# Sixteen transposed tiles, single sign tiles and a new reckoning of the order in a four-layer graph network

## The chip, the cores and the metric

The kernel runs on one core of a Trainium2 chip. The metric is the time of one execution on the device, in microseconds (us). The time before is the median of three runs.

## The reference

Sixteen graphs of 1024 nodes with 64 features go through four residual layers. Each layer normalises its input, applies a ReLU and adds what a graph layer makes of it, with the same adjacency matrix `adj` of 1024 x 1024 each time (about 0.8% of it off the diagonal is not zero). Layers 0, 1 and 2 use dense products with `adj`; layer 2 uses it twice. Layer 3 asks only which neighbours a node has, thins the list of nodes with more than ten, and takes a weighted sum of three quantiles over what is left.

```python
h = relu(layernorm(x)); x = x + einsum(einsum(adj, h), W0)                 # layer 0: one product with adj
h = relu(layernorm(x)); m = relu(relu(h @ W1 + b1) @ W2 + b2)              # layer 1
msg = relu(einsum(adj, m)); x = x + GRU(msg, h)                            #   one product with adj
h = relu(layernorm(x)); T1 = einsum(adj, h); T2 = 2 * einsum(adj, T1) - h  # layer 2: two products with adj
x = x + (K0 * h + K1 * T1 + K2 * T2) @ weight + bias
h = relu(layernorm(x)); adj_d = dilate_adj(adj, mask)                      # layer 3
agg = sum(w * quantile(h of the neighbours in adj_d, tau)) over tau = 0.25, 0.5, 0.75
x = x + (relu((h + agg) @ W1 + b1) @ W2 + b2) * mask
```

## The kernel before

The work of a graph goes through several Python generators, each of which yields operations one after the other (`run`, L1333). A planner, `Weave`, takes all generators side by side and decides in which order the operations are issued. On the chip each engine then works through its own queue in that order, and semaphores make it wait for results of the others. The planner's time is a reckoning only: `Line.cost` (L306) gives each operation a cost, for which it takes its engine, and a delay (`later`) after which its result is there. `Weave.run` (L432) picks the engine that can start something first, and on it, among the operations that could start within `SLACK` = 0.1 us of that, the one whose generator has the lowest key. An operation's key holds for all that its generator issues, DMA loads on SP's queue included.

The generators, for graph b:

- `transposing` (L862), key b - 3: loads eight column blocks of `adj` (512 KB each, on SP's queue, two `block` buffers), transposes each in eight 128 x 128 pieces on PE, and has ACT copy the two PSUM banks into one tile of the stock `AT`. Eight `AT` tiles hold the transposed matrix of one graph. The stock has `AT` = 15 of them.
- `coding` (L664), key b + `CODE_KEY` = b - 3: takes the sign of each `AT` tile on ACT (fp16, tile `there`, two signs in one tile), clears the diagonal on DVE, and packs the neighbours of each node into words by matmuls. The words go through the tile `words`, are transposed and become `code`.
- `lists` (L696), key b - 2: makes each node's list of up to 24 neighbours from `code`, mostly on DVE (`MAX8`, `MATCH_REPLACE8`), and thins it.
- `layers` (L927), key b - 3: layers 0 to 2 and the norm of layer 3. It has four passes over the eight `AT` tiles (`into`, L937; sixteen matmuls a pass). The fourth pass gives each `AT` tile back, once its sign has been taken. Two generators `layering` (L1116) share the graphs, even and odd, and graph b begins when graph b - 1 has done its first pass. At the end the results go into a tile of the stock `pay` (3 tiles), and from there into the DRAM tensors `table` and `rows`, both on SP's queue. Behind them in that queue come the load of the next `X` (two tiles) and further blocks.
- `gathering` (L1122), key b + 1: 80 indirect DMAs on POOL (10 neighbours x 8 tiles of nodes) that read rows of `table` into one of two tiles `G`.
- `quantiling` and `dense` (L1151, L1264), keys b + 1 and b: a sorting network on DVE over the gathered cells, weights on DVE and ACT, the two small matrix products on PE, the store of the output, and the return of the `pay` tile.

After graph 15 the few nodes with longer lists are taken together (`MANY`, 122 gathers in four groups, then 9 scatters).

Of the kernel before, what the change touches and what calls it, by code (L numbers as in the profile page):

```python
# [10 lines left out]
F32 = mybir.dt.float32  # L11
F16 = mybir.dt.float16
# [4 lines left out]
AF = mybir.ActivationFunctionType  # L17
# [5 lines left out]
P = 128  # L23
N = 1024
NT = N // P
C = 64
NB = 64
S = N // NB
# [70 lines left out]
EXTRA = 6 * NT  # L99
BIG = 1e30  # L100
SLACK = 0.1
GATHER = 1.33
RANK = 3.0
SHARE = 3
LONGEST = 512
AT = 15
XTILES = 2
PAYS = 3
LIST_KEY = -2
CODE_KEY = -3  # L110
WORDS = NB - 1
LAYERS = 5
CAND = WORDS + 8 * LAYERS
UNIT = 2.0 ** -10
# [65 lines left out]
def network(n, places, beam=200):  # L180
# [4 lines left out]
    for layer in needed(batcher(n), range(places)):  # L185
        new = {}
        for buf, (cost, ops) in states.items():
            classes = {}
            for a, b, la, lb in layer:
# [73 lines left out]
class Op:  # L263
# [5 lines left out]
    def __init__(self, line, make, writes, reads, cost, later=0.0, after=()):  # L269
        self.line, self.make, self.cost, self.later, self.after = line, make, cost, later, after  # L270
        self.writes, self.reads = [place(a) for a in writes], [place(a) for a in reads]
# [16 lines left out]
class Line:  # L288
# [17 lines left out]
    def cost(self, method, out, reads, kwargs):  # L306
        if method == "dma_start":
            return 0.4, 2.0 + out.nbytes() / 150e3
        n = max(a.free_size() for a in [out] + reads)
        extra = "accum_out" in kwargs  # L310
        if self.name == "DVE":
            fixed = {"match_replace": 0.145, "max": 0.155}.get(method, 0.155)
            return fixed + n / 960 + 0.08 * extra, 0.0
        if self.name == "ACT":
            scalars = sum(hasattr(kwargs.get(k), "ap") for k in ("bias", "scale"))
            return 0.225 + n / 1400 + 0.09 * scalars + 0.19 * extra, 0.0
        if self.name == "PE":
            if method == "transpose":
                return 0.19, 0.25
            n = out.free_size()  # L320
            if mybir.dt.size(reads[0].dtype) == 2:
                return 0.06 + n / (4400 if out.shape[0] == C else 2200), 0.3
            pair = n == 512 and reads[0].shape[0] == P and out.shape[0] == C
            return (0.58 if pair else max(0.34, 0.06 + n / 545)), 0.3
        return 1.33, 2.2


class Weave:
# [13 lines left out]
    def stock(self, name, tiles):  # L342
        self.stocks[name] = list(tiles)

    def give(self, name, t):
        self.stocks[name].append(t)
# [121 lines left out]
class Fast:  # L468
# [4 lines left out]
    def __init__(self, tc, half, whole, weights):  # L473
# [107 lines left out]
        def stock(name, count, shape, dtype=F32):  # L581
            weave.stock(name, [p.tile(shape, dtype, name=f"{name}{i}") for i in range(count)])
# [6 lines left out]
        weave.stock("fm", banks[5:8])  # L589


        stock("there", 2, [P, 2, N], F16)
        stock("code", 1, [P, NT, NB])
        self.words = p.tile([P, 512], F32, name="words")
        self.top = p.tile([P, NT, WORDS], F32, name="top")
        self.cand = p.tile([P, NT, CAND], F16, name="cand")
        stock("L", 3, [P, NT, LIST], F16)
# [3 lines left out]
        stock("block", 2, [P, NT, P])  # L601
        stock("AT", AT, [P, N])
        stock("X", XTILES, [P, NT, C])
# [27 lines left out]
    def gather(self, out, table, at, reads):  # L631

        def make():
            return self.nc.gpsimd.indirect_dma_start(  # L634
                out=out, out_offset=None, in_=table, in_offset=bass.IndirectOffsetOnAxis(ap=at, axis=0))
        return Op(self.G, make, [out], [reads, at], GATHER, 2.2)

# [26 lines left out]
    def coding(self):  # L664

        V, T, S = self.V, self.T, self.S
        for b in range(GRAPHS):
            yield float(b) + CODE_KEY
            yield lambda: self.turns > 0
            bank = yield "bits"  # L670
            turned = self.turned[b]
            for j in range(0, NT, 2):
                there = yield "there"
                for i in range(2):
                    yield lambda: len(turned) > j + i
                    yield S.activation(there[:, i, :], turned[j + i], AF.Sign)
                self.masked[b] = j + 2
                own = there.rearrange("p i (t m) -> p (i t) m", m=P)[:, j:j + NT + 2:NT + 1, :]
                yield V.tensor_mul(own, own, self.noteye[:, None, :].to_broadcast([P, 2, P]))
                for i in range(2):  # L680
                    for half in range(2):
                        yield T.matmul(bank[half * NB:(half + 1) * NB, :], self.bits[:, (j + i) * NB:(j + i + 1) * NB],
                                       there[:, i, 512 * half:512 * half + 512], start=j + i == 0, stop=j + i == NT - 1)
                self.weave.give("there", there)
            yield S.activation(self.words, bank, AF.Identity, bias=self.low, scale=1.0 / UNIT)
            self.weave.give("bits", bank)
            bank = yield "tp"
            for q in range(4):
                yield T.transpose(bank[:, q * P:(q + 1) * P], self.words[:, q * P:(q + 1) * P], self.ident)
            code = yield "code"  # L690
            yield S.activation(code.rearrange("p (h q) w -> p q h w", h=2),
                               bank.rearrange("p (q h w) -> p q h w", h=2, w=NB), AF.Copy)
            self.weave.give("tp", bank)
            self.coded[b] = code
# [95 lines left out]
    def longest(self):  # L790
# [5 lines left out]
        for _ in range(3):  # L796
            tiles.append((yield "AT"))
        run = tiles[0][:, 0:BINS * Q]
# [59 lines left out]
        for t in tiled:  # L858
            self.weave.give("AT", t)


    def transposing(self, adj):  # L862

        D, T, S = self.D, self.T, self.S
        blocks = {}


        early = self.early

        def load(i):  # L870
            b, j = divmod(i, NT)
            blocks[i] = block = early.pop(0).rearrange("p (t m) -> p t m", m=P) if 2 <= i < NT else (yield "block")
            queue = self.A if i % 2 and i < NT else D
            yield queue.dma_start(block, adj[b, :, j * P:(j + 1) * P].rearrange("(t p) m -> p t m", p=P))

        total = GRAPHS * NT
        yield -1.0
        for i in range(NT):
            yield from load(i)
        for i in range(total):  # L880
            b, j = divmod(i, NT)
            yield float(b) - 3
            if NT <= i + 1 < total:
                yield from load(i + 1)
            block = blocks.pop(i)
            at = yield "AT"
            for half in range(2):
                bank = yield "tp"
                for q in range(4):
                    yield T.transpose(bank[:, q * P:(q + 1) * P], block[:, 4 * half + q, :], self.ident)  # L890
                yield S.activation(at[:, 512 * half:512 * half + 512], bank, AF.Copy)
                self.weave.give("tp", bank)
            if not 2 <= i < NT:
                self.weave.give("block", block)
            self.turned[b].append(at)
# [31 lines left out]
    def layers(self, w, b, x):  # L927
# [9 lines left out]
        def into(bank, h, last=False):  # L937

            def step(j):
# [6 lines left out]
                if last:  # L946
                    yield lambda: self.masked[b] > j
                    give("AT", turned[j])
            return step
# [575 lines left out]
def general_layers(tc, b, x, adj, nodemask, VT, mB, X, H, maskT, c16, ident, ones16, ones_row, eps,  # L1525
# [3 lines left out]
    with tc.tile_pool(name="g1", bufs=1) as p1, tc.tile_pool(name="g2", bufs=2) as p2, \  # L1529
# [16 lines left out]
        def neighbours(g):  # L1546
            AT = p2.tile([P, NT, N], F32, name="AT")
            CN = p1.tile([P, NT, N], F16, name="CN")
# [434 lines left out]
```

## Time and profile before

| | |
|---|---|
| median of three runs | 2125.57 us (2113.96 to 2135.73) |
| the profiled execution | 2138.34 us, its span 2136.4 us |
| granted PE clock over the span | 0.782 |
| first gather of graph 0 | 130.9 us after the start |
| last gather of graph 15 | 1898.0 us |
| waits of DVE for `X` loads | 81.4 us, 16 times |
| POOL's gathers | 1402, 0.94 us each in the median |

The profile gives busy times for each engine: PE (matmuls), PEld (weight loads, which overlap PE), DVE, ACT and POOL. SP only issues DMAs. Matrix products in fp32 stand in the trace as two instructions each. A line of the timeline gives the start in us, the length, the engine, the source line, the operation, the tiles written and read (without their numbers), their shape, how many such instructions were merged, and in brackets how long the engine was idle before and what it is thought to have waited for. Nearly all operations carry L303, the line of the planner's wrapper, so they are told apart by their tiles. The clock column is the share of full speed that PE was granted.

### The profile page before, as it was taken

To read this page: it belongs to the slowest core of one execution; us is meant where nothing else is said; L and a number is where in the kernel's file an instruction comes from. 1 tells how busy PE (TensorE), PEld (TensorE's weight loads), DVE (VectorE), ACT (ScalarE), POOL (GpSimd) and SP (SyncE) were. 2 spreads that over 40 slices of the span, in tenths; PEclk is the share of its full clock that TensorE was granted. 3 is DMA by queue.
4 is the path that set the end of the run, shared out by engine and by line. 5 is a ranking of instruction groups with operands and counts; after the bars stand their busy time and mean duration, and the time that the engine had idled before them with its cause. 6 is when DMAs were issued, how large, how long until landed. Compare 5 with 4: busy or idle time off the path is not lost. (4 is left out here: it accounts for less than half of the span.)

```text
span 2136.4 us, 22993 instructions
## 1 busy us (share of the span) xinstructions
PE 1533.9 (72%) x6172; PEld 717.0 (34%) x6172; DVE 1632.9 (76%) x4293; ACT 1073.5 (50%) x2921; POOL 1437.7 (67%) x1441
## 2 busy tenths in 40 slices
PE   6978677869787879787887878787978872233303
PEld 2443323333434343343333333334343331111302
DVE  2661687978888887888886969787788899949646
ACT  3654647566666655566656474757466532011000
POOL 2047776777676767577777667676757777776772
PEclk9979796978788796989796979787779786555555
DMA  4242625252625252444334353525252314121110
GB/s 121 70 86 57 117 38 94 59 105 52 104 51 104 52 93 58 58 94 61 88 62 94 50 94 61 104 48 99 51 92 50 43 31 41 30 31 24 32 27 11
DMA packets 246840, 140.93 MB, mean 66 GB/s; under 512 B 76048, under 2 KB 223952, under 8 KB 246704
## 3 DMA queue, kind: packets, MB, share of 16 engines
q1 hardware_dynamic: 195664, 88.11, 18.4%
q0 software_dynamic: 46096, 48.62, 17.5%
q10 hardware_dynamic: 4944, 2.66, 0.5%
q8 instruction: 53, 0.87, 0.2%
q14 instruction: 83, 0.68, 0.1%
HBM read 120.10 MB, written 19.17 MB: 65 GB/s over the span
## 5 line engine op out<-in xcount | busy, mean ns | idle before, releaser
L634 POOL DMA_INDIRECT G<-table,pay x1402 | 1408.0, 1004 | 652.6 <-issue 351.6
L303 PE MATMUL bank<-AT,nodes 128*64 128x512 f32 x2048 | 605.7, 671 | 88.1 <-ACT nodes L303 78.6
L303 PEld LDWEIGHTS bank<-AT,nodes 128*64 128x64 f32 x2048 | 181.6, 153 | 386.2 <-issue 223.6
L303 PE MATMUL bank<-G,c 128*128 128x512 f32 (+3 forms) x382 | 172.1, 590 | 183.4 <-DVE G L303 179.4
L303 PE MATMUL bank<-c,block 128*128 128x128 f32 x976 | 223.5, 349 | 106.8 <-DMA block<-in_adj 60.5
L303 ACT ACTIVATE AT<-bank 128x512 f32<-128x512 f32 x256 | 149.5, 588 | 188.9 <-PE bank L303 186.4
L303 PEld LDWEIGHTS bank<-c,block 128*128 128x128 f32 x976 | 147.3, 176 | 229.2 <-issue 137.7
L303 DVE TENSOR_TENSOR G<-G 128x512 f32<-128x512 f32 (+3 forms) x313 | 200.1, 674 | 2.8
L303 ACT ACTIVATE nodes<-X,off,ri 128x64 f32<-128x64 f32 x360 | 141.0, 429 | 42.6 <-DVE off L303 41.3
L303 DVE TENSOR_TENSOR net<-G 128x512 f32<-128x512 f32 (+6 forms) x240 | 150.6, 672 | 11.3 <-ACT G L303 9.3
L303 PEld LDWEIGHTS bank<-G,c 128*128 128x128 f32 x382 | 72.1, 226 | 254.5 <-DVE G L303 129.1
L303 ACT ACTIVATE G<-G,coef 128x64 f32<-128x64 f32 x384 | 98.2, 336 | 110.0 <-DVE coef L303 109.8
L303 ACT ACTIVATE sq<-X,st 128x64 f32<-128x64 f32 x360 | 124.6, 346 | 49.7 <-DVE st L303 34.1
L303 ACT ACTIVATE there<-AT 128x1024 f16<-128x1024 f32 x128 | 132.1, 1050 | 0.9
L303 ACT ACTIVATE wide<-bank 64x512 f32<-64x512 f32 x128 | 75.1, 586 | 108.7 <-PE bank L303 107.5
L303 DVE TENSOR_TENSOR G<-net 128x512 f32<-128x512 f32 (+7 forms) x189 | 117.2, 667 | 0.7
L303 DVE TENSOR_TENSOR G<-G,net 128x512 f32<-128x512 f32 (+3 forms) x177 | 111.4, 679 | 0.9
L303 PE MATMUL bank<-wide,wg 64*64 64x512 f32 (+1 forms) x192 | 110.1, 656 | 0.8 <-ACT wide L303 0.4
L303 DVE SCALAR_TENSOR_TENSOR G<-bad,G 128x512 f32<-128x512 f32 (+1 forms) x176 | 109.8, 693 | 0.0
L303 DVE MAX8 L<-cand 128x8 f16<-128x103 f16 x384 | 91.9, 263 | 8.8
L303 PE MATMUL bank<-there,c 128*64 128x512 f16 x256 | 79.8, 449 | 24.3 <-DVE there L303 24.1
L303 DVE TENSOR_REDUCE st<-X 128x8 f32<-128x512 f32 x48 | 32.9, 686 | 82.5 <-DMA X<-in_x 81.4
(200 smaller groups left out, 2235.0 us busy)
## 6 DMA issues: line engine op xcount, KB each, us to landing
block<-in_adj SPq DMA_DIRECT2D x121, 512.0 KB, 4.2
G<-table,pay POOLq DMA_INDIRECT x1402, 2.8
rows<-pay SPq DMA_DIRECT2D x16, 632.0 KB
table<-pay SPq DMA_DIRECT2D x16, 264.0 KB, 5.2
X<-in_x SPq DMA_DIRECT2D x16, 256.0 KB, 8.5
out<-yo SPq DMA_DIRECT2D x16, 256.0 KB, 2.6
G<-in_adj SPq DMA_DIRECT2D x3, 512.0 KB, 10.7
G<-in_adj ACTq DMA_DIRECT2D x3, 512.0 KB, 9.2
```

Of the source, the lines that this page charges most:

```text
L303: return Op(self, lambda: f(*args, **kwargs), writes, reads, cost, later)
L634: return self.nc.gpsimd.indirect_dma_start(out=out, out_offset=None, in_=table, in_offset=bass.IndirectOffsetOnAxis(ap=at, axis=0))
```

## The change

The stock `AT` grows from 15 to 16 tiles of 4 KB per partition. The stock `there` goes from two tiles for two signs each to three tiles for one sign each, and `words` is no longer a tile of its own but borrows one of `there`. Signs, masking and matmuls then go tile by tile, with a masking multiply for each tile in place of one for each pair.

The planner reckons most operations shorter: with DVE and ACT the time until the result is there moves out of the cost into the delay. On PE transposes and fp32 products get cheaper, and a gather goes from 1.33 to 1.29. The key of `coding` goes from b - 3 to b - 2, that of `transposing` from b - 3 to b - 2.5; all others stay.

```diff
-GATHER = 1.33
+GATHER = 1.29
...
-AT = 15
+AT = 16
...
-CODE_KEY = -3
+CODE_KEY = -2
...
         if self.name == "DVE":
-            fixed = {"match_replace": 0.145, "max": 0.155}.get(method, 0.155)
-            return fixed + n / 960 + 0.08 * extra, 0.0
+            fixed = {"match_replace": 0.165, "max": 0.095}.get(method, 0.07)
+            return fixed + n / 960 + 0.08 * extra, 0.09
         if self.name == "ACT":
             scalars = sum(hasattr(kwargs.get(k), "ap") for k in ("bias", "scale"))
-            return 0.225 + n / 1400 + 0.09 * scalars + 0.19 * extra, 0.0
+            return 0.13 + n / 1400 + 0.09 * scalars + 0.19 * extra, 0.1
         if self.name == "PE":
             if method == "transpose":
-                return 0.19, 0.25
+                return 0.165, 0.25
...
-            return (0.58 if pair else max(0.34, 0.06 + n / 545)), 0.3
+            return (0.51 if pair else max(0.26, 0.06 + n / 640)), 0.3
...
-        stock("there", 2, [P, 2, N], F16)
+        stock("there", 3, [P, N], F16)
         stock("code", 1, [P, NT, NB])
-        self.words = p.tile([P, 512], F32, name="words")
...
-            for j in range(0, NT, 2):
+            for j in range(NT):
                 there = yield "there"
-                for i in range(2):
-                    yield lambda: len(turned) > j + i
-                    yield S.activation(there[:, i, :], turned[j + i], AF.Sign)
-                self.masked[b] = j + 2
-                own = there.rearrange("p i (t m) -> p (i t) m", m=P)[:, j:j + NT + 2:NT + 1, :]
-                yield V.tensor_mul(own, own, self.noteye[:, None, :].to_broadcast([P, 2, P]))
-                for i in range(2):
-                    for half in range(2):
-                        yield T.matmul(bank[half * NB:(half + 1) * NB, :], self.bits[:, (j + i) * NB:(j + i + 1) * NB],
-                                       there[:, i, 512 * half:512 * half + 512], start=j + i == 0, stop=j + i == NT - 1)
+                yield lambda: len(turned) > j
+                yield S.activation(there, turned[j], AF.Sign)
+                self.masked[b] = j + 1
+                own = there[:, j * P:(j + 1) * P]
+                yield V.tensor_mul(own, own, self.noteye)
+                for half in range(2):
+                    yield T.matmul(bank[half * NB:(half + 1) * NB, :], self.bits[:, j * NB:(j + 1) * NB],
+                                   there[:, 512 * half:512 * half + 512], start=j == 0, stop=j == NT - 1)
                 self.weave.give("there", there)
-            yield S.activation(self.words, bank, AF.Identity, bias=self.low, scale=1.0 / UNIT)
+            there = yield "there"
+            words = there.bitcast(F32)
+            yield S.activation(words, bank, AF.Identity, bias=self.low, scale=1.0 / UNIT)
...
-                yield T.transpose(bank[:, q * P:(q + 1) * P], self.words[:, q * P:(q + 1) * P], self.ident)
+                yield T.transpose(bank[:, q * P:(q + 1) * P], words[:, q * P:(q + 1) * P], self.ident)
+            self.weave.give("there", there)
...
-            yield float(b) - 3
+            yield float(b) - 2.5
```

## The prediction

> **What bounds the kernel now.** I read the busy times first, then the gather queue, then the stretch between two graphs. The page names no full engine:
>
> ```profile
> PE 1533.9 (72%) x6172; PEld 717.0 (34%) x6172; DVE 1632.9 (76%) x4293; ACT 1073.5 (50%) x2921; POOL 1437.7 (67%) x1441
> L634 POOL DMA_INDIRECT G<-table,pay x1402 | 1408.0, 1004 | 652.6 <-issue 351.6
> ```
>
> POOL is nearer its limit than 67% says: of its 652.6 us idle, 351.6 are the 0.3 us between two gathers that wait for nothing. Gathers in full flow start 1.25 us apart. The longer waits stand where a graph's gathers begin, as between graphs 3 and 4 (POOL's timeline):
>
> ```profile
> 556.46 0.95 POOL L634 DMA_INDIRECT G<-table,pay  x1 [0.30 <-ACT sq L303]
> 566.65 0.94 POOL L634 DMA_INDIRECT G<-table,pay  x1 [9.25 <-DVE below L303]
> ```
>
> The releaser named is wrong: SP issued graph 4's store of `table` at 560.21, such a store lands 5.2 us later, and the gathers follow. Graph by graph, the 80 gathers begin at 130.9, 231.2, 342.8, 452.1, 566.7, 676.1 and so on to 1792.5 (graph 15). That is 1661.6 us for 15 steps, 110.8 each. From first to last, one graph's gathers take 99.0 us in graph 0 and 103.8 on average in graphs 1 to 15; with one interval of 1.25 a step could take 105. The sum of what is lost between graphs is 93 us. So the layers, which end with the table, set the pace, not POOL.
>
> What sets the layers' pace shows in ACT's timeline, at the evictions into `AT` (sixteen to a graph, two to a tile; those of graph 6 run from 561.4):
>
> ```profile
> 618.64 0.57 ACT L303 ACTIVATE AT<-bank 128x512 f32<-128x512 f32 x1
> 620.68 0.58 ACT L303 ACTIVATE AT<-bank 128x512 f32<-128x512 f32 x1
> ...
> 653.05 0.60 ACT L303 ACTIVATE AT<-bank 128x512 f32<-128x512 f32 x1 [9.99 <-PE bank L303]
> 654.76 0.60 ACT L303 ACTIVATE AT<-bank 128x512 f32<-128x512 f32 x1
> ```
>
> Graph 6's seventh tile is done at 621; its eighth stands for 32 us, until graph 5's fourth pass on PE (from 642.78) gives its first tile back. With 15 tiles, 8 + 7 are all there is. Graph 6's first pass needs the eighth tile, so its second, third and fourth passes come after graph 5's fourth, and graph 7's eighth tile after those. The eighth tiles of graphs 5 to 8 come at 544.2, 653.0, 765.3, 881.9: 109 to 117 apart, the step of the gathers. This is a closed loop through one missing tile.
>
> The rows by gather period (length, then PE, PEld, DVE, ACT and POOL busy, clock) show that no engine is full:
>
> ```profile
> 130.90:231.20 100.30, 79.14 (x322) 38.24 (x322) 37.82 (x153) 57.09 (x147) 75.88 (x81) 0.77 0.44 81
> 566.70:676.10 109.40, 90.51 (x368) 41.90 (x368) 91.72 (x244) 67.86 (x185) 80.24 (x80) 0.84 0.40 77
> 787.00:904.90 117.90, 99.15 (x365) 42.26 (x364) 92.16 (x247) 69.53 (x196) 78.32 (x80) 0.78 0.41 72
> ```
>
> DVE has 17.7 us idle in the second row, ACT 41.5.
>
> **The change, part by part.** *Sixteenth `AT` tile.* It adds 4 KB per partition; `there` shrinks from 8 to 6 KB and `words` (2 KB) goes, so space is even. Graph 6's sixth tile was finished at 612, its seventh at 618.6 to 621, 6.6 us on. An eighth at that spacing comes at 627 instead of 653: 26 us earlier. From X load (561.3) to table (781.3) graph 6 took 220 us, two graphs in flight; 220 - 26 = 194, or 97 per step. Three others are late next. POOL: 105, above. The `pay` tiles: graph 3's output store is issued at 738.0, 294.9 after its table (443.1), landing takes 2.6, and graph 6 first writes that tile 14.1 before its own table; 311.6 over three graphs is 103.9. DVE: 91.7 of work, plus whatever in-order waits remain. If all 17.7 us of them remain, the step stays at 109.4 and nothing is won. So the gain lies between 0 and 93. I take 62 (a step of 106.7, DVE idle down to 15): DVE's dependable waits, such as 81.4 us over the run for the X loads, remain, but much of the rest is waiting on chains that the loop itself held back.
>
> *Signs in single tiles.* The signs stay 128. The masking multiplies go from 64 of 128x256 (287 ns, 18.4 us busy) to 128 of 128x128. Their price lies between that of a 128x64 subtraction (`more<-more,top`, 220 ns) and 287: 28 to 37 us, so +10 to +18 over the run. I take 13, nearer to the smaller shape, 0.8 per graph, inside DVE's idle; uncovered it costs 13. The words borrow a `there` tile from eviction to the last of four transposes; code 5 was out at 556.9 and graph 6's first sign came at 577.9, so nobody waits: 0, or up to 5 per graph if signs then follow at once (I take 0).
>
> *New reckoning.* It changes no instruction's length, only the order on each in-order queue. It comes closer to what runs:
>
> ```profile
> 612.57 2.53 DVE L303 TENSOR_TENSOR G<-G 128x512 f32<-128x512 f32 x4
> ```
>
> Four take 2.53 and one 0.69, so they start 0.61 apart. The old reckoning says 0.688, the new 0.603 and 0.09 to the result. By the old one DVE's 244 instructions of a graph look some 20 us longer than they are, and the order is laid out around a full DVE that isn't full. No row shows the new order. The kind of wait that an order makes or removes is DVE's for `ri<-sd` (66.7 us over the run, 37 times), so I bound the edit by 67 won and 67 lost, and take 0: such waits lie in DVE's idle, which isn't the limit while tables come late.
>
> *Later keys.* Transposing moves behind its own graph's layers (b - 2.5 against b - 3), with its SP block loads; coding falls to b - 2. Behind a delayed sign on ACT nobody critical is queued; behind code b waits list b on DVE, and behind that the `pay` of graph b. For graph 5 the list is done at 593.0 and `pay` first written at 655.0: 62 us of cover. Price 0; without cover, microsecond for microsecond. The head (first gather 130.9) and the tail (238 us from graph 15's last gather to the end) I leave alone; the two final gather periods hold 7.7 + 26.1 us of idle DVE to take work pushed into them, so the tail could cost up to 34, or give 13.
>
> *Two rules.* Graph 0's gathers ran 1.253 us apart with DVE busy 37.8 of 100.3, the later ones 1.314 with DVE at about 91. The Trainium skill (SBUF — State Buffer, "SBUF: two separate sides") has it that certain DVE instructions lock GpSimd out of a shared port while it writes descriptors for gathers. By that rule a denser DVE would not leave POOL at its best pitch: 1.253 would make the step 100, while the row's 1.314 makes the 105 I use. Second, PE ran at clock 0.50 from 564 to 598, after a wait of 7.49 us for a block load, then at 1.00. The skill (TensorE: Matmul & The Clock Gate, Part 1) says idle of about 3.4 us halves the clock; by it no single price for a matmul, old or new, can be right on both sides of such a gap. The change doesn't remove the X and block loads behind each table, so I count on no better clock.
>
> **Sum.** The profiled execution took 2138.3 (span 2136.4); the median of three is 2125.6, or 0.994 of it. 2138.3 - 62 = 2076.3; times 0.994 is 2064.
>
> **Rivals.** *The step is held by lists (slower).* Coding falls behind layers, transposing and older work, signs slip on ACT, and `pay` waits for the list. With tables 26 us earlier the cover is 36, and the chain is back at 220 once signs slip by 62; beyond that it is slower than now. At 70 it is 194 + 34 = 228: a step of 114, +3.2 x 15 = +48, 2173 in the median's scale. For: three edits push coding back. Against: ACT idles 41.5 a graph, and eight signs need 8.4.
> *DVE and `pay` take over at once.* Quantiles rank last; if the output lags 16 us more, 327.6/3 = 109.2 per step: -24, or about 2102. For: 103.9 leaves little room. Against: part of the lag is waiting.
> *It doesn't do what it says.* The eighth tile is planned behind the other graph's fourth pass anyway, now that transposing ranks lower: no gain, 2126. Against: PE was idle 5.12 us at 627, and the planner fills idle time.
>
> **How the numbers follow.** A measurement can't tell less than 1% (2104 to 2147) from no change. Forecast 62%: 2064, own range 2020 (93 + 13 won) to 2100. DVE and `pay`: 16%, half of it faster by 1%, half within. Not done: 6%. Lists: 16%. Faster 0.70, same 0.14, slower 0.16. The range of 2015 to 2135 holds all cases but the slower one, the 67 lost by order included (2131); of the 67 won it leaves the last 18 out.
>
> **What would show it.** The eighth tile within 10 us of the seventh; tables some 107 apart; waits at a graph's first gather falling from 93 to about 30 in sum; DVE still about 92 a graph. I am wrong if the step stays at 110 with the eighth tile early (then look at lists, `pay` and DVE's idle), or if the tail after graph 15's last gather grows by tens of microseconds.

## The result, and the profile after

The changed kernel takes 2182.31 us in the median of four runs (2178.42 to 2189.26), beside 2126.7 (2113.96 to 2135.73) for the one before: 1.027 of it, 95% interval 1.0208 to 1.0332. The forecast was 2064, in a range of 2015 to 2135. It was wrong in sign.

The profiled execution took 2186.15 us with a span of 2184.2, 47.8 more than before (2136.4). The starts of the gathers divide the difference:

| us | before | after | |
|---|---|---|---|
| first gather of graph 0 | 130.9 | 141.4 | +10.5 |
| 15 steps, from there to graph 15's first gather | 1661.6 | 1704.4 | +42.8 |
| from there to the end | 343.9 | 338.4 | -5.5 |
| in the steps: waits between two graphs, sum | 93.1 | 58.1 | -35.0 |
| in the steps: first to last gather, sum over graphs 0 to 14 | 1549.8 | 1627.5 | +77.7 |

The two rows on the steps leave out one interval of 1.25 us per step. So what stood between the graphs shrank, as forecast, though not as far as to 30. What the forecast didn't have is that the gathers of one graph now take longer from the first to the last. The gathers themselves got no longer (995 ns in the mean, before 1004): over graphs 0 to 14 the waits beyond the usual 0.3 us between a graph's first and last gather sum to 89 us, before 4.

The stores of `table` divide the 47.8 in another way. The first is 10.1 us later, the 15 steps from there to graph 15's table take 1659.2 us (before 1649.9), and graph 15's gathers begin 51.2 behind their table (before 17.3). So the layers lose little pace, 9.3 us in 15 steps, and most of the loss is that the gathers fall behind the tables.

The page's busy times and gather row of the changed kernel:

```profile
PE 1570.6 (72%) x6172; PEld 683.8 (31%) x6172; DVE 1638.3 (75%) x4357; ACT 1077.4 (49%) x2924; POOL 1425.5 (65%) x1441
L633 POOL DMA_INDIRECT G<-table,pay x1402 | 1395.4, 995 | 711.3 <-issue 344.7
```

DVE works 5.4 us more over the run, POOL 12 less, and POOL is idle 59 us more. Where it waits stands in POOL's timeline, at three gathers with a long wait in brackets. The first begins graph 4, the second graph 8; the third comes after the first eight of graph 9:

```profile
572.08 0.98 POOL L633 DMA_INDIRECT G<-table,pay  x1 [9.11 <-DVE G L303]
...
1030.25 1.15 POOL L633 DMA_INDIRECT G<-table,pay  x1 [13.94 <-DVE net L303]
...
1174.73 0.97 POOL L633 DMA_INDIRECT G<-table,pay  x1 [20.08 <-PE bank L303]
```

SP's timeline has the tables of graphs 8 and 9, and after them the output store of graph 7:

```profile
1015.12 0.37 SPq L639 DMA_DIRECT2D table<-pay  x1
...
1123.43 0.37 SPq L639 DMA_DIRECT2D table<-pay  x1
...
1232.32 0.38 SPq L639 DMA_DIRECT2D out<-yo  x1
```

Graph 4's gathers follow their table (store issued at 565.9) by 6.2 us, as before. Graph 8's table was issued at 1015.1, and the gathers come 15.1 later; graph 9's wait 20 us after the first eight, until 51 after their table. They wait for the tile `G`, which the quantiles of two graphs earlier still use: graph 7's output is not stored before 1232.3. On average over graphs 2 to 14 the gathers begin 20.7 us behind the table's store (before 6.4) and the output is stored 303.4 behind it (before 283.9).

The evictions into `AT` in ACT's timeline, the last of graph 6:

```profile
664.24 1.06 ACT L303 ACTIVATE AT<-bank 128x512 f32<-128x512 f32 x2
669.58 1.05 ACT L303 ACTIVATE AT<-bank 128x512 f32<-128x512 f32 x2
672.38 0.60 ACT L303 ACTIVATE AT<-bank 128x512 f32<-128x512 f32 x1 [0.47 <-PE bank L303]
673.83 0.59 ACT L303 ACTIVATE AT<-bank 128x512 f32<-128x512 f32 x1
```

The eighth tile is done 4 us after the seventh (before, 34 us). But the eighth is not earlier: it ends at 674, and ended at 655 before (107 us behind the load of its graph's `X`, before 94). The seventh, which ended at 621, has moved back to 671. The hole was filled from the wrong side.

The gather periods of graphs 0, 4 and 6 (length, then PE, PEld, DVE, ACT and POOL busy, clock):

```profile
141.40:241.90 100.50, 81.99 (x320) 35.12 (x319) 40.02 (x160) 56.93 (x147) 76.09 (x81) 0.79 0.41 80
572.10:675.80 103.70, 87.44 (x351) 36.56 (x350) 85.89 (x239) 64.29 (x176) 78.14 (x81) 0.88 0.39 76
789.90:910.90 121.00, 100.35 (x400) 44.05 (x398) 92.24 (x252) 75.09 (x210) 78.53 (x80) 0.87 0.45 85
```

Graph 6's period is 121.0 long with DVE at work for 92.2, so DVE stands idle for 28.8. The waits that DVE's idle time is put down to (us in total, times, longest), before:

```profile
DVE st L303 <- DMA X<-in_x: 81.4, 16, 7.9
DVE ri L303 <- ACT sd L303: 66.7, 37, 9.0
DVE cand L303 <- ACT cand L303: 37.2, 13, 3.8
...
DVE there L303 <- ACT there L303: 35.2, 9, 15.6
...
DVE of_h L303 <- ACT wide L303: 23.8, 6, 10.4
```

And after:

```profile
DVE there L303 <- ACT there L303: 78.8, 29, 16.6
DVE st L303 <- DMA X<-in_x: 76.8, 15, 8.1
DVE of_h L303 <- ACT wide L303: 58.6, 11, 15.1
DVE ri L303 <- ACT sd L303: 49.1, 19, 8.8
```

DVE's waits for a sign on ACT have doubled, and so has the gated layer's wait (`of_h`); the waits for `ri` and `cand` went down. In the 14 steps from graph 1 to graph 15 DVE was busy 1291.8 of 1561.3 us before, and 1309.5 of 1603.9 after: 18 us more work in that stretch and 25 us more idle.

### The profile page after: what moved, and what is told of

Its sections match the earlier page's. It is cut to its first block, busy times and chain, and to the rows that moved or that the text cites. A ratio compares the mean times of both kernels' runs of the same rounds, so it can differ in the third digit from the quotient of the medians.

```text
span 2184.2 us, 23009 instructions
## 1 busy us (share of the span) xinstructions
PE 1570.6 (72%) x6172; PEld 683.8 (31%) x6172; DVE 1638.3 (75%) x4357; ACT 1077.4 (49%) x2924; POOL 1425.5 (65%) x1441
## 5 line engine op out<-in xcount | busy, mean ns | idle before, releaser
L633 POOL DMA_INDIRECT G<-table,pay x1402 | 1395.4, 995 | 711.3 <-issue 344.7
L303 PE MATMUL bank<-AT,nodes 128*64 128x512 f32 x2048 | 638.2, 664 | 91.4 <-ACT AT L303 73.1
L303 PE MATMUL bank<-G,c 128*128 128x512 f32 (+3 forms) x382 | 196.3, 648 | 210.2 <-DVE G L303 207.8
L303 PEld LDWEIGHTS bank<-AT,nodes 128*64 128x64 f32 x2048 | 168.1, 149 | 395.6 <-issue 210.9
L303 PE MATMUL bank<-c,block 128*128 128x128 f32 x976 | 196.3, 315 | 30.7 <-DMA block<-in_adj 20.1
L303 PEld LDWEIGHTS bank<-c,block 128*128 128x128 f32 x976 | 119.8, 155 | 231.8 <-issue 186.8
L303 ACT ACTIVATE nodes<-X,off,ri 128x64 f32<-128x64 f32 x360 | 147.3, 429 | 46.7 <-DVE off L303 46.3
L303 PE MATMUL bank<-wide,wg 64*64 64x512 f32 (+1 forms) x192 | 102.3, 620 | 3.4 <-ACT wide L303 3.2
L303 PE MATMUL bank<-c,nodes 128*64 128x128 f32 x128 | 42.9, 361 | 68.0 <-ACT nodes L303 67.4
```

Source lines behind the costliest of these rows:

```text
L303: return Op(self, lambda: f(*args, **kwargs), writes, reads, cost, later)
L633: return self.nc.gpsimd.indirect_dma_start(out=out, out_offset=None, in_=table, in_offset=bass.IndirectOffsetOnAxis(ap=at, axis=0))
```

## The experiments

Each part of the change was first run alone, and then taken out of the whole. A ratio is always to the kernel before on the same chip, with its 95% interval. The planner's own end, which some expectations use, is the time at which its reckoning lets the last operation finish: 2106 for the kernel before and 1989 for the changed one. Nine runs and their kernels before (3271 to 3314 us) fell on a second kind of chip, on which the kernels took half as long again. Its ratios are compared with one another only, and set beside the others only in one table, where they are marked.

**The sixteenth tile and the single signs alone.** Keys and reckoning are those of before.

```diff
-AT = 15
+AT = 16
...
-        stock("there", 2, [P, 2, N], F16)
+        stock("there", 3, [P, N], F16)
```

> The kernel before with the sixteenth AT tile and the single sign tiles alone; old reckoning, old keys. Theory K (the lower keys make the transposes late): the loop through the missing tile is open and nothing else is changed, so 2064 to 2100, with the eighth tile within 10 us of the seventh and a gather step of 106 to 109. Theory R (the new reckoning lays out a worse order): the same, 2064 to 2100. Theory T (the tiles themselves cost, by the extra masking multiplies or the borrowed words): about 2180. If the loop never was the bound, 2127.

Measured: 2173.31 us, 1.0227 (1.0175 to 1.0278). This is the trial of the forecast's main step, and it falls. ACT's timeline, the two evictions of graph 6's eighth tile:

```profile
653.01 0.60 ACT L303 ACTIVATE AT<-bank 128x512 f32<-128x512 f32 x1
656.84 0.60 ACT L303 ACTIVATE AT<-bank 128x512 f32<-128x512 f32 x1 [0.38 <-PE bank L303]
```

And the loads and stores about that graph in SP's timeline, its `X` load and its table, each behind an older table:

```profile
567.41 0.37 SPq L639 DMA_DIRECT2D table<-pay  x1
567.83 0.57 SPq L639 DMA_DIRECT2D rows<-pay  x1
568.46 0.70 SPq L303 DMA_DIRECT2D X<-in_x  x1
...
783.22 0.37 SPq L639 DMA_DIRECT2D table<-pay  x1
783.63 0.58 SPq L639 DMA_DIRECT2D rows<-pay  x1
784.26 0.83 SPq L303 DMA_DIRECT2D X<-in_x  x1
```

The `X` load of graph 6 is issued 1 us behind the table of graph 4, because one generator (`layering`) issues both, one after the other. In the kernel before it is 1.0 to 1.2 us in every graph; in the others it can be more, up to 15. So "from X load to table" is nearly two table steps by construction, whatever limits them: 783.22 - 567.41 = 215.8 here, over two steps. I had read these 220 us as a chain in which a late tile shows up one for one. The means over graphs 2 to 14 of several kernels show that it doesn't (us, from the starts in each trace):

| kernel | X load to 8th tile | 8th tile to table | X load to table | table to output store |
|---|---|---|---|---|
| before | 96.0 | 125.9 | 221.9 | 283.9 |
| tiles alone | 73.6 | 148.5 | 222.1 | 290.4 |
| keys alone | 110.9 | 110.4 | 221.3 | 282.3 |
| reckoning without PE alone | 98.3 | 126.0 | 224.3 | 275.7 |
| PE's prices alone | 93.0 | 137.7 | 230.7 | 326.6 |
| whole reckoning alone | 97.7 | 131.4 | 229.1 | 324.1 |
| whole change, old prices for PE | 112.8 | 111.3 | 224.1 | 274.5 |
| whole change | 105.8 | 115.2 | 221.0 | 303.4 |

With the sixteenth tile alone the eighth comes 22.4 us earlier in the mean, close to the 26 of the forecast, and what follows it takes 22.6 longer. Graph 6, shown above, is among those that gain least: its eighth tile ends 89 us behind the `X` load, before 94. With the keys alone the eighth comes 14.9 later, and what follows takes 15.5 less. The table stays where it is, counted from the `X` load. The waits of DVE that grow most with the tiles alone are those for `ri`, 100.8 us (before 66.7), and for `there`, 83.7 (35.2). That they make up the 48 us is not shown. Theory T alone had this time (about 2180), but of its two causes the multiplies take only 10.4 us more, and the borrowed words keep no sign waiting: ACT is never idle for more than 0.1 us before one. Nor were the sixteenth tile and the single signs run apart, so which of the two costs is open.

**The new reckoning alone.** Costs and delays of DVE, ACT and PE and `GATHER` as in the change; tiles and keys of before.

```diff
-            fixed = {"match_replace": 0.145, "max": 0.155}.get(method, 0.155)
+            fixed = {"match_replace": 0.165, "max": 0.095}.get(method, 0.07)
...
-            return (0.58 if pair else max(0.34, 0.06 + n / 545)), 0.3
+            return (0.51 if pair else max(0.26, 0.06 + n / 640)), 0.3
```

> The kernel before with the new reckoning alone (costs of DVE, ACT, PE and gather). Theory R: about 2180, since the order is laid out for engines that run faster than they do: the planner's own end falls from 2106 to 1991 while the chip follows by nothing. Theories K and T: 2100 to 2140, as before.

Measured: 2240.37 us, 1.0531 (1.0473 to 1.059), the dearest part. Its planner's end was 1991. Theory R had the cause and put the time at 2180. DVE was busy 1627.3 us (before 1632.9), and the products with `AT` took PE 613.9 (605.7), so the loss is waiting; the gathers start 32.9 us behind the tables on average, and a step takes 118.1.

**The two keys alone.**

```diff
-CODE_KEY = -3
+CODE_KEY = -2
...
-            yield float(b) - 3
+            yield float(b) - 2.5
```

> The kernel before with the two keys alone (transposing b - 2.5, coding b - 2). Theory K: about 2180 (2160 to 2200), with the transposes of a graph spread over some 80 us in place of 60 and its last one 15 to 20 us later. Theories R and T: 2110 to 2140.

Measured: 2198.7 us, 1.0343 (1.0292 to 1.0393), as theory K had it. The first gather comes at 143.2 (before 130.9) and the waits between graphs sum to 142.9 (93.1). The lists, at which my rival looked, are not late: from graph 1 on they are done 28 to 54 us before `pay` is first written.

**The whole change without the keys.** In a first form the planner issued the first writers of graph 1's `code` before the last reader of graph 0's.

> The changed kernel with the two old keys (b - 3 both). Theory K: 2064 to 2120, all of the loss gone. Theories R and T: 2170 to 2200, nothing gone.

Measured: 26226.65 us. The count of lists that don't fit came out above zero, and the kernel then runs its general version behind the fast one. Nothing about the keys can be read from it. The second form gives `code` back after its last reader, and was run three times, each time on a chip of the second kind:

```diff
-        self.weave.give("code", code)
         found = self.small("found")
         yield V.tensor_tensor(found, code[:, :, WORDS], cnt, op=ALU.not_equal)
         yield V.tensor_reduce(self.over_column(), found, axis=AX.X, op=ALU.max)
+        self.weave.give("code", code)
```

> The changed kernel with the two old keys, and with the code tile given back one operation later, after its last reader. In e_nokeys the planner issued graph 1's code before the check of graph 0's list had read the old one, the check reported a list too long, and the general kernel ran behind the fast one; that run says nothing on the keys. Theory A: 2125 + 48 + 115, about 2290. If the new keys are a remedy for the new reckoning: above 2182, near the 2240 of the reckoning alone. Theory S: 2150 to 2240.

> The changed kernel with both keys as before (coding and transposing at b - 3), the tile code given back after its last reader: the sixteen tiles and the whole new reckoning. So far, beside about 2127 before: tiles alone 1.023, reckoning alone 1.053, keys alone 1.034, all three 1.027. Theory 'the keys take back what the reckoning costs' (transposing that ranks behind its own graph's layers leaves PE to the layers): without them 1.05 to 1.08, 2235 to 2290, and the first write of pay within 1 us of the output store it waits for, as with the reckoning alone. Theory 'the sixteenth tile takes it back' : 1.00 to 1.03, 2130 to 2190. Theory 'parts add up': 1.076, 2288. The planner's own end is 2005 for it.

> The same kernel as e_nokeys3 (tiles and reckoning, both keys at b - 3), once more, since that call fell on the chip on which all kernels take half as long again (1.065 there). On a chip like that of the other runs, beside the whole change's 1.027 and the reckoning alone at 1.053. Theory 'the keys take back what the reckoning costs': 1.045 to 1.08, 2225 to 2295. Theory 'the sixteenth tile takes it back': 1.00 to 1.03, 2130 to 2190. Theory 'parts add up': 1.076.

Measured: 3482.36, 3528.22 and 3485.96 us, ratios 1.0641 (1.059 to 1.0693), 1.0654 (1.0598 to 1.071) and 1.0646 (1.0573 to 1.0718). In the last of them the first write of `pay` comes within 0.6 us of the output store it waits for in every graph, and the gathers begin 56 to 65 us behind the tables through the middle of the run.

**The whole change without the new reckoning** (tiles and keys), on chips of the second kind as well:

> The changed kernel with the old reckoning (sixteen tiles, single signs, new keys). Alone the tiles cost 48 us and the keys 74. Theory A (the parts cost each by itself and add): 2125 + 48 + 74, about 2247. Theory P (with the old reckoning the chip follows the planner's own end, 22 to 52 us behind it; the planner ends at 2165 here): 2187 to 2217. Theory S (the kernel before has an order picked out of many, and any other order lies some per cent above it without a cause in its parts): 2150 to 2240, no sum.

> The sixteen tiles with single signs and the two later keys, with the old reckoning throughout. Theory 'with the old reckoning the chip follows the planner's end' (2106 gave 2127, 2118 gave 2173, 2175 gave 2199, so 21 to 55 above it): its end is 2165, so 2186 to 2220, 1.028 to 1.044. Theory 'parts add up': 1.057, 2248. Theory 'tiles mend the late transposing of the later keys' (eight tiles can be filled at once): 1.00 to 1.02, 2127 to 2170.

Measured: 3328.53 and 3357.98 us, 1.0189 (1.0124 to 1.0254) and 1.0137 (1.0084 to 1.019). `pay` always has 28 us or more to spare there.

**The whole change without the tiles** (reckoning and keys), on the same chip as the second of these:

> The new reckoning and the two later keys, with fifteen AT tiles and signs in pairs as before. Theory 'the keys take back what the reckoning costs': 1.01 to 1.035, 2150 to 2200. Theory 'the sixteenth tile takes it back': 1.05 to 1.09, 2235 to 2315. Theory 'parts add up': 1.087, 2312. The planner's own end is 1999 for it, 10 above the whole change; if only the planner's end counted it would stay within 1% of the whole change, 2160 to 2205.

Measured: 3428.75 us, 1.0372 (1.031 to 1.0434); the first write of `pay` comes within 0.5 us of the output store in nine of 13 graphs. On these chips the pairs therefore rank 1.014 (no reckoning), 1.037 (no tiles), 1.065 (no keys). That is what one would see if the later keys take back part of what the reckoning costs. But neither the single parts nor the whole change were run on such a chip, and set beside one another alone the three pairs don't exclude parts that add up. So this stays a pointer.

**Is it any other order that costs?** Two changes of the reckoning with no purpose, each made in the kernel before: `SLACK` and the gather's price.

```diff
-SLACK = 0.1
+SLACK = 0.11
```

> The kernel before with SLACK 0.11 in place of 0.10, a second shuffle without meaning (planner's end 2113). Theory S: 2140 to 2200. Theories A and P: 2120 to 2150.

```diff
-GATHER = 1.33
+GATHER = 1.34
```

> The kernel before with GATHER 1.34 in place of 1.33: an edit without meaning, which only shuffles the order (planner's end 2107 against 2106). Theory S: 2140 to 2200, as slow as the parts of the change. Theories A and P: 2115 to 2140, as before.

> The kernel before with GATHER 1.34 in place of 1.33 once more, since the chip of the first run ran all kernels at 3270 us. Theory S (the order of before is picked out of many): 2140 to 2200. Otherwise 2115 to 2145.

Measured: `SLACK` 3270.23 us, 0.9998 (0.9971 to 1.0026), and the gather's price 3275.19, 0.9996 (0.9969 to 1.0022), both on a chip of the second kind; the gather's price again on an ordinary one 2129.23, 1.0005 (0.9976 to 1.0035). So a small change of the reckoning doesn't cost as such. But the two hardly shuffle. DVE's instructions can be put in a row as each trace has them, told apart by operation and tile names without numbers, with masks and words left out. So many of 4229 then stand elsewhere than in the kernel before (a move from one graph to another can go unseen):

| kernel | moved on DVE | ratio |
|---|---|---|
| the gather's price 1.34 | 0 | 1.0005 (second kind of chip: 0.9996) |
| `SLACK` 0.11 (second kind of chip) | 209 | 0.9998 |
| PE's prices 5% dearer (second kind of chip) | 363 | 1.0059 |
| reckoning without PE alone | 517 | 1.0115 |
| tiles alone | 681 | 1.0227 |
| whole change | 695 | 1.027 |
| keys alone | 697 | 1.0343 |
| whole change, four `pay` tiles | 711 | 1.0424 |
| whole change, old prices for PE | 747 | 1.0275 |
| whole reckoning alone | 850 | 1.0531 |
| PE's prices alone | 1032 | 1.0535 |

The pairs on the second kind of chip fit in: 678 moved and 1.014 to 1.019 without the reckoning, 774 and 1.037 without the tiles, 860 and 1.064 to 1.065 without the keys. Whatever the edit, the loss grows with the distance from the old order, though not strictly. So theory S stands in a weaker form: the kernel before may have an order picked out of many, from which any large departure costs. No run here tests that, since none moves as much with an edit that has no purpose.

**Which price?** PE's new prices alone, then all the others alone, then the whole change with PE's old ones.

```diff
-                return 0.19, 0.25
+                return 0.165, 0.25
...
-            return (0.58 if pair else max(0.34, 0.06 + n / 545)), 0.3
+            return (0.51 if pair else max(0.26, 0.06 + n / 640)), 0.3
```

> The kernel before with the new PE prices alone (transposes 0.165, fp32 products 0.51 and from 0.26); the planner's end is 2070, its PE total 1321 us where the chip's PE is busy 1534. Theory PE (of the new reckoning it is the PE prices that harm: the chip's PE, at the clock it is granted, needs the old ones, so the order promises PE results that come late and the other engines stand in line behind them): 2180 to 2240, as the whole reckoning. Theory DA (it is the shorter DVE and ACT): 2110 to 2145.

> The kernel before with the new reckoning of DVE, ACT and gathers, PE as before; the planner's end is 2018. Theory PE: 2060 to 2140, the harm of the reckoning gone. Theory DA: 2180 to 2240.

> The changed kernel with the old PE prices; the planner's end is 2069 against 1989. Theory PE: 2090 to 2150, most of the loss of 57 gone. Theory DA: 2170 to 2200. If the tiles or the keys hold the changed kernel whatever the prices: 2170 to 2200 too.

Measured: PE's prices alone 2247.51 us, 1.0535 (1.0468 to 1.0602); the others alone 2155.71, 1.0115 (1.0051 to 1.0178); the whole change with PE's old prices 2191.63, 1.0275 (1.0206 to 1.0345). PE's prices alone cost as much as the whole reckoning, as theory PE had it; but the others alone lie above its range (2060 to 2140), and the whole change with the old prices lies where the tiles or the keys would hold it. POOL's waits with them (us in total, times, longest):

```profile
POOL G L634 <- DVE net L303: 175.6, 11, 36.4
```

Graph 3 shows the longest of these, in POOL's timeline:

```profile
482.05 1.15 POOL L634 DMA_INDIRECT G<-table,pay  x1 [36.35 <-DVE net L303]
```

Its gathers wait for the quantiles of graph 1 to leave `G`. SP's timeline, an output store and the table behind it,

```profile
1023.44 0.38 SPq L640 DMA_DIRECT2D out<-yo  x1
1038.54 0.37 SPq L640 DMA_DIRECT2D table<-pay  x1
```

and the write of `pay` on DVE between the two,

```profile
1023.48 0.24 DVE L303 TENSOR_SCALAR pay<-c 128x8 f32<-128x8 f32 x2
```

show the write 0.04 us behind the store. The quantiles have fallen 43 us further behind the tables (326.6 against 283.9 in the table above), and both `G` and `pay` come free too late. The trace of the kernel before also says what a product costs on PE:

```profile
L303 PE MATMUL bank<-AT,nodes 128*64 128x512 f32 x2048 | 605.7, 671 | 88.1 <-ACT nodes L303 78.6
```

Two instructions make one product, so these are 1024 products at 0.59. The old price was 0.58, the new one 0.51. The old prices add up to about 1530 us over the kernel, the new ones to about 1320, and PE was busy for 1533.9.

And yet PE's old prices do not help the whole change. With them the gathers sit right behind the tables again (6.4 us), and the output store 274.5 behind the table. But the eighth tile comes 112.8 us after the `X` load, as with the keys alone, and the waits between graphs rise to 155.3. The 15 table steps take 1704.8 us (whole change 1659.2, before 1649.9), and graph 15's gathers begin 11.9 behind their table (51.2, before 17.3). The loss changes its place, not its size.

**PE's prices the other way**, 5% dearer, on a chip of the second kind.

```diff
-                return 0.19, 0.25
+                return 0.1995, 0.25
...
-            return (0.58 if pair else max(0.34, 0.06 + n / 545)), 0.3
+            return (0.6090 if pair else max(0.3570, 0.06 + n / 519)), 0.3
```

> Before with PE's transposes and fp32 products reckoned 5% dearer (0.1995; 0.609 and 0.357), nothing else. Theory 'a price for PE below what the chip grants does the harm, one above does none': PE busy in the trace is as long as the old prices say, so there is no more to win or lose than 1%: 2106 to 2148. Theory 'with the old DVE prices the chip follows the planner's end': its end is 2168 (before 2106), so 2189 to 2223, 1.03 to 1.045. Theory 'any change of order costs, whichever its direction': over 1.015.

Measured: 3325.87 us, 1.0059 (1.003 to 1.0088): within the 1% of the first theory, and against the planner's end as a guide, though on another kind of chip than expected. It also moves DVE's order far less than the cheaper prices do (363 against 1032), so it doesn't tell whether the direction or the distance counts.

**Is it the `pay` loop?** In the changed kernel the first write of `pay` comes within 1 us of the output store ahead of it in six of 13 graphs. A fourth `pay` tile takes that wait away.

```diff
-AT = 16
+AT = 15
...
-PAYS = 3
+PAYS = 4
...
-        stock("there", 3, [P, N], F16)
+        stock("there", 2, [P, N], F16)
```

> The whole change, with four pay tiles in place of three and, to make room for the fourth, fifteen AT tiles and two single there tiles. It asks whether the loop through pay (output of graph b stored, tile given back, tables of graph b + 3 written into it) is what holds the changed kernel, in whose trace the first write of pay comes within 1 us of the output store from graph 5 on. Theory 'pay holds it': with a fourth tile the write waits for nothing, a step falls towards 108 and the kernel to 0.99 to 1.01 of before. Theory 'the lag of the quantiles behind the tables holds it, pay only passes it on': the gathers still start 15 to 50 us behind the tables and DVE still ends last, 1.02 to 1.04. Theory 'the fifteenth tile matters': above 1.04. On a chip on which every kernel takes half as long again it is to be set beside the reckoning and the keys without the tiles, 1.037: the first theory says 1.00 to 1.02 there, the second 1.03 to 1.045.

Measured: 2219.98 us, 1.0424 (1.0374 to 1.0475). The write now runs up to 27 us ahead of the store that it would have waited for, and the kernel isn't faster. The output store falls further behind the table, 317.6 us in the mean of graphs 2 to 14 (303.4). POOL's waits, first the kernel before, then the changed one (where L633 is the same line):

```profile
POOL G L634 <- PE bank L303: 13.9, 36, 3.2
...
POOL G L633 <- PE bank L303: 92.9, 41, 21.2
POOL G L633 <- DVE net L303: 52.2, 4, 17.1
```

Then with four `pay` tiles:

```profile
POOL G L633 <- PE bank L303: 133.3, 44, 35.7
...
POOL G L633 <- DVE net L303: 46.1, 4, 18.3
```

The gathers wait for `G` instead. So `pay` only passes on that the quantiles are late. That the same holds for `G` is argued, since no tile was added there. This kernel also has one `AT` and one `there` tile less, and part of the 1.5% by which it is behind the whole change may be theirs: by its number it lies on the edge between the theory of the lag and that of the fifteenth tile.

## Why the prediction was wrong, point by point

**The missing tile as the pace.** "26 us earlier ... 220 - 26 = 194" is the step that failed. The tile did come 22.4 us earlier when it was added alone, and the table came no earlier, since the rest took 22.6 longer. The tables then came 111.2 us apart (before 110.0), the sign of being wrong that the prediction had named. In the whole change the tile came even later than before, 105.8 us behind the `X` load in place of 96.0. A stretch that begins with a load issued right behind the table of two graphs earlier is two steps long by construction. It says nothing of which part of it sets its length. That eighth tiles came "109 to 117 apart, the step of the gathers" said as little: everything in a periodic schedule comes a step apart.

**The new reckoning at 0, bounded by 67 both ways.** Alone it costs 2240.37 - 2125.1 = 115 us. I took the bound from DVE's largest order wait, `ri<-sd`; the loss shows elsewhere, in quantiles that finish 40 us later behind their table, and so in `G` and `pay`. I also looked at DVE's prices, which did come closer to what runs, and passed over PE's, which left it: 0.59 measured, 0.58 replaced by 0.51. The reason given for 0, that such waits lie in DVE's idle while tables come late, failed with it: the waits for `ri` hardly moved (64.4 us, before 66.7).

**Later keys at 0.** Alone they cost 2198.7 - 2125.1 = 74 us. The cover that I named, 62 us of the lists, was real and was not used up. I had looked at coding; in the trace the transposes come late, with the eighth tile 14.9 us later behind the `X` load and the first gather at 143.2, and the `X` loads are issued up to 14 us behind the table of two graphs earlier (before 1.2 at most). Which of these sets the loss isn't shown. Neither key was run alone, so which of them does it is open.

**Signs in single tiles.** The multiplies went from 64 at 287 ns to 128 at 227, 18.4 to 29.0 us: +10.6, where I had 13. That "nobody waits" because the words borrow a tile holds: ACT is never idle for more than 0.1 us before a sign, neither with the tiles alone nor in the whole change. What the forecast didn't have is that DVE's waits for the signs rise, by 48.5 with the tiles alone.

**Head and tail.** The tail is right: 237.4 us from graph 15's last gather, before 238.4. The head is 10.5 late. The keys alone make it 12.3 late, the reckoning without PE 11.3, the tiles 0.8; the whole reckoning alone makes it 1.0 early.

**DVE's idle "down to 15" a graph.** It was 19.3 in the 14 steps before and is 21.0 now. That it was waiting which the loop held back isn't borne out.

**The gathers' pitch.** The step of 105 took 1.314 us between gathers, by the row of a busy DVE. That held: outside graph 0 a gather takes 1.00 us in the mean before and after, in graph 0 0.95, with a median of 0.94 or 0.95 throughout. What stretched a graph's gathers is waiting for `G`. Whether DVE's work makes the few long gathers was not tried.

**The rivals.** "Lists" has the nearest time, 2173, and the wrong mechanism: lists keep 27 us or more. "DVE and `pay` take over at once" has the mechanism closest to what the trace shows, with the output lag 19.5 us longer (I had 16), but put the price on the wrong side of zero.

**What is shown and what is not.** Shown: an earlier eighth tile alone doesn't shorten the step; PE's prices alone cost as much as the whole reckoning; each of the three parts costs by itself, and they don't add (48 + 115 + 74 = 237, together 56); four `pay` tiles don't help. Not settled: what does set the step of the kernel before, which part takes back the others' loss on ordinary chips, and why PE's old prices win nothing in the whole change. Nor is it settled whether PE's prices do harm because they lie below what PE takes, or because they move the order furthest. What in the order puts the quantiles behind when PE is reckoned too cheap was not traced to single instructions; that the planner counts on PE being free when it isn't, and orders DVE by that, is only argued. No version was found that beats the kernel before.

## What to carry to other kernels

Before a chain is taken for the one that sets the pace, look whether its start is triggered by its own end some steps earlier: then its length is the period times a whole number, and only an experiment that moves one link shows whether the rest follows. Where a planner lays out in-order queues, check each engine's prices against the busy time that the trace shows, and don't take a shorter plan for a shorter run: PE's prices below that time took the plan from 2106 to 2070 us and the run from 2129 to 2248. It is no remedy by itself, since the old prices won nothing back in the whole change. A control edit that is to stand for "any other order" should move as much of the order as the edit under test. When gathers or stores wait for a tile, add a tile as a trial before calling it the cause: a late user can make a buffer look short.

## What the runs showed of the hardware

Some chips run the kernel before in 3271 to 3314 us in place of 2127. DVE's and ACT's instructions last as long there as elsewhere (DVE busy 1625.4 us with `SLACK` at 0.11, before 1632.9; ACT 1084.9 and 1073.5); the gaps between certain DVE instructions don't. The groups with `MAX8` and `MATCH_VALUE_LOAD`, of which the lists are made (busy, mean ns, then idle before them), in the kernel before on an ordinary chip:

```profile
L303 DVE MAX8 L<-cand 128x8 f16<-128x103 f16 x384 | 91.9, 263 | 8.8
L303 DVE MATCH_VALUE_LOAD cand<-L,cand 128x8 f16 x256 | 23.6, 92 | 8.7
```

And with `SLACK` at 0.11, which is as fast as the kernel before, on one of those chips:

```profile
L303 DVE MAX8 L<-cand 128x8 f16<-128x103 f16 x384 | 91.7, 263 | 454.9 <-remote 338.7 <-issue 85.1 <-DVE cand L303 29.5
L303 DVE MATCH_VALUE_LOAD cand<-L,cand 128x8 f16 x256 | 23.6, 92 | 295.8 <-remote 152.5 <-DVE L L303 78.7 <-issue 62.7
```

In one list's stretch gaps of 0.8 to 3.2 us stand before most of them. The idle time before the two groups is 733 us longer, and the span, 3267.7, is 1131 longer. What the gaps are, the trace doesn't say (its releasers are inferred), nor were the other 398 us looked into.

With PE's new prices alone the granted clock fell to 0.761 from 0.782, and PE waited 93.3 us for blocks (before 60.5), the longest 10.7. The Trainium skill (TensorE: Matmul & The Clock Gate, Part 1) has idle times of about 3.4 us halve the clock, which goes the same way; no run separates what that is worth. It can't be much of the loss by PE's own time: PE was busy 1542.9 us, 9 more than before, in a run 119 us longer.
